# Two gathers per step of a graph-attention loop, issued behind another copy on the same engine

## The chip, the cores and the metric

The kernel runs on one core of a Trainium2 chip. A core has five engines with a queue of instructions each: PE (matrix products), DVE (elementwise work), ACT (activation functions and copies), POOL (GpSimd, which also issues the gathers) and SP (which here only issues transfers). An engine works through its queue in the order in which the program wrote it, and waits on semaphores for the others. The metric is the time of one execution on the device, in microseconds (us), lower being better. The kernel before takes 810.82 us, the median of three runs between 807.87 and 810.95.

## What is computed

Two layers of graph attention over 2048 nodes for 8 batches, a residual and two layer norms. The graph is one adjacency matrix `adj`, the same for all batches, sparse, and densest at its first nodes. Cut to what matters:

```python
def _gat_layer(h, mask, b):
    scores = jnp.einsum('...nd,...md->...nm', h, h)
    scores = jnp.where(mask, scores, NEG)
    attn = jax.nn.softmax(scores, axis=-1)
    return jnp.einsum('...nm,...md->...nd', attn, h) + b

mask = graph + jnp.eye(N) > 0
h = jnp.einsum('bnc,hdc->bhnd', x, Wh)               # B 8, N 2048, H 4 heads, D 64
out_h = _gat_layer(h, mask[None, None], bh)          # layer 1, per head
z = leaky_relu(concat_of_heads(out_h), 0.2)
h2 = jnp.einsum('bnk,dk->bnd', z, Wo)
out2 = _gat_layer(h2, mask[None], bo)                # layer 2, one head
out = layernorm(leaky_relu(out2, 0.2)) * gamma + beta
x = layernorm(x + out)
```

## The kernel before, in words

The kernel uses that the graph is sparse. The first 59 nodes (the hubs) are attended densely. The other 1989 nodes stand in 153 sets of 13. For each set a list of up to 128 neighbour nodes (one column of the tile `index`) is found on the chip from the adjacency matrix. Everything that a set needs of its neighbours is then fetched by one **gather** (`gather`, line 907; its instruction carries line 912): an indirect transfer from a table in device memory, 128 rows of 520 float32, issued by POOL, which spends its own time on it.

Before layer 1 comes a stage of dense hub work, in which the lists of the first sets are made as well. Layer 1 is the loop of line 1272. Its step `i` does two sets, 77 steps in all, software-pipelined: within one pass the work of several steps stands side by side. What matters here, in the order of the code:

- `scores(i + 1)`, line 941: PE multiplies the turned neighbours with the set's own maps; DVE subtracts the mask (line 946), ACT takes the exponential (line 953).
- `values(i)`, line 967: PE multiplies the exponentials with the gathered rows `rows[1, 2i]` and `rows[1, 2i+1]`. After it these two buffers are free. There are ten such buffers (`ROWS = 10`), so the gathers of step `i + 5` (`LOOK = 5`) use the buffers that `values(i)` has just read.
- **the two gathers** of step `i + 5`, lines 1298 to 1300.
- `own_rows`, line 920, in even steps: POOL copies the own nodes' inputs `xo`, used two steps later.
- `more(1)`, line 1318, while there are pieces left, which is in steps 0 to 9: a piece `raw` of the adjacency matrix is loaded over SP's queue (lines 776 and 778), POOL turns it to `a` (line 783) and sets a few elements (line 788, in every second step). The lists of the last 45 sets are made of these.
- `second_maps(i - 2)`, PE, line 1001; `second_rows`, `columns` and so on.
- `keep_own(i - 2)`: DVE copies the second layer's own maps out of PSUM (line 1006), and **POOL copies them into the big tile `own`** (line 1007). That tile is read in layer 2 only.
- `keep_rows(i - 3)`, DVE line 1015 and a transfer on SP's queue (line 1018) into the table of layer 2.
- the turning of the gathered rows of step `i + 3`, PE line 571 into `bank`, in two halves of four transposes with line 984 between them. This is the first reader of a gather's data. The pair issued in step `i` is thus first read at the end of step `i + 2`.

No scheduler moves anything here: the order of the code is the order on each engine. Layer 2 follows as a loop of its own with gathers from the second table. If the numbers leave the limits, a slower general kernel runs behind; it doesn't here.

Of the kernel before, what the change touches and what calls it, by code (L numbers as in the profile page):

```python
# [361 lines left out]
def fast_kernel(ctx: ExitStack, tc: tile.TileContext, x, adj, Wh, bh, Wo, bo, gamma, beta, out, flag):  # L362
# [14 lines left out]
    NG = (NS + 1) // 2  # L377
# [25 lines left out]
    def set0(g):  # L403
        return min(2 * g, NS - 2)
# [46 lines left out]
    table1 = dram.tile([N, ROW], F32, name="table1")  # L451
# [121 lines left out]
    def leaky(cat, n, name):  # L573

        z = work.tile([P, HP, 2, n], F32, tag="z", name=name, bufs=3)
        for hp in range(HP):
            nc.scalar.activation(z[:, hp], cat[:, :, hp * n:(hp + 1) * n], AF.Identity, bias=bhp[:, hp:hp + 1], scale=1.0)  # L577
        return z
# [5 lines left out]
    def project(ot, cat, n):  # L584

        for hp in range(HP):
            for s in range(2):
                for j in range(2):
                    h = 2 * hp + j
                    nc.tensor.matmul(cat[half(j), s, hp * n:(hp + 1) * n], whT[half(s), h * D:(h + 1) * D],  # L590
                                     ot[half(s), h, :], start=True, stop=True)
# [132 lines left out]
    def hub_heads(v, cat):  # L724

        for hp in range(HP):
            for s in range(2):
                for j in range(2):
                    h = 2 * hp + j
                    nc.tensor.matmul(cat[half(j), s, FREE + hp * HUB:FREE + (hp + 1) * HUB], whT[half(s), h * D:(h + 1) * D],  # L730
                                     oth[half(s), h, v * HUB:(v + 1) * HUB], start=True, stop=True)

    def keep_hub_heads(v, cat):
        for hp in range(HP):
            nc.scalar.activation(zh[:, hp, :, v * HUB:(v + 1) * HUB], cat[:, :, FREE + hp * HUB:FREE + (hp + 1) * HUB],
                                 AF.Identity, bias=bhp[:, hp:hp + 1], scale=1.0)
# [164 lines left out]
    def place(s):  # L901
        return (s + 1) % NS
# [4 lines left out]
    def gather(table, s, layer, new):  # L907
        t = rows[layer, s] = new(f"g{layer}_{s}")
        if layer == 1:
            s = set0(s // 2) + s % 2  # L910
        bound = {} if layer == 2 and place(s) < RING else dict(bounds_check=N - 1, oob_is_err=False)
        nc.gpsimd.indirect_dma_start(out=t.rearrange("n q c -> n (q c)"), out_offset=None, in_=table,  # L912
                                     in_offset=bass.IndirectOffsetOnAxis(ap=index[:, s:s + 1], axis=0), **bound)
# [20 lines left out]
    def scores(g, sp):  # L934
        xt = held.pop(("T", 1, g)).rearrange("c j (q n) -> c j q n", q=Q)
        y = held["y", g // 2][:, g % 2 * GM:(g % 2 + 1) * GM, :].rearrange("p n h -> p (n h)")
        for j in range(2):
            for q in range(Q):
                for p in range(2):
                    for r in range(2):  # L940
                        nc.tensor.matmul(sp[half(r), p, (q * 2 + j) * M:(q * 2 + j + 1) * M], xt[half(p), j, q, half(r)],  # L941
                                         y[half(p), (j * Q + q) * M:(j * Q + q + 1) * M], start=True, stop=True)

    def weigh(g, sp):
        e = es[g % 2]
        nc.vector.tensor_tensor(e[:, :16 * M].rearrange("p (a q n) -> p a q n", a=2, q=Q),  # L946
                                sp[:, :, :8 * M].rearrange("p a (q n) -> p a q n", q=Q),
                                mask[:, set0(g):set0(g) + 2, :].rearrange("p s n -> p (s n)").unsqueeze(1).unsqueeze(1)
                                .to_broadcast([P, 2, Q, 2 * M]), OP.subtract)
# [53 lines left out]
    def keep_own(g, ph):  # L1003

        t = held["own", g] = work.tile([P, GM], F32, tag="own", name=f"own{g}")
        nc.vector.tensor_copy(t, ph)  # L1006
        nc.gpsimd.tensor_copy(own[:, :, set0(g) * SET:(set0(g) + 2) * SET].rearrange("c q (j n) -> c j q n", j=2),  # L1007
                              t.rearrange("c (j q n) -> c j q n", j=2, q=Q))
# [81 lines left out]
    LOOK = 5  # L1090
# [77 lines left out]
    def one(name, tag):  # L1168
        return psum1.tile([P, 2, 512], F32, tag=tag, name=name)
# [102 lines left out]
    for i in range(-3, NG + 3):  # L1272
        if 0 <= i + 1 < NG:
            sp = one(f"s{i + 1}", "S")
            scores(i + 1, sp)
            weigh(i + 1, sp)
        cat = one(f"cat{i}", "C") if i <= NG else None
        if i > NG:
            cat = one(f"cat{i}", "S" if i == NG + 1 else "C")
        ph, pr = cat[:, 0, 384:384 + GM], cat[:GM, 1, 384:512]  # L1280
        if 0 <= i - 1 < NG:
            project(held.pop(("ot", i - 1)), cat, GM)
            if i in hub_heads_at:
                hub_heads(hub_heads_at[i], cat)
            held["z", i - 1] = leaky(cat, GM, f"z{i - 1}")
            if i in hub_heads_at:
                keep_hub_heads(hub_heads_at[i], cat)
        if 0 < i + 2 < NG:
            t = held["T", 1, i + 2] = work.tile([P, 2, 512], F32, tag="xTg", name=f"xTg{i + 2}", bufs=3)
            for k in range(2):  # L1290
                nc.scalar.copy(t[:, k, :], bank[k])  # L1291
        if 0 <= i + 1 < NG:
            lift(i + 1)
        if 0 <= i < NG:
            op = one(f"o{i}", "O")
            values(i, op)
            invert(i, op)
        if 0 <= i + LOOK < NG and i > -3:
            for j in range(2):
                gather(table1, 2 * (i + LOOK) + j, 1, rows_tile)  # L1300
        if NG - LOOK <= i < NG - 1:
            for j in range(2):
                k = 2 * (i - NG + LOOK) + j
                hub_block(k, rows_tile(f"gh{k}"))
        if i + 6 < NG and i % 2 == 0 and i >= -2:
            own_rows((i + 6) // 2)
        if i == 20:
            nc.gpsimd.memset(xbs[1], 1.0)
        if i % 2 == 0 and 0 <= (i - 30) // 2 <= NV:
            load_own((i - 30) // 2)  # L1310
        if 0 <= i - 1 < NG:
            leak(held["z", i - 1])
        if i in (4, 8):
            leak(zh)
        if i >= 0:
            if turns():
                some(1)
            more(1)
            if todo3 and i == todo3[0][0]:
                r = todo3.pop(0)[1:]  # L1320
                make_keys(*r, late_two)
                if r == (1, 1):
                    picks += pick(1)
                    done = 2 * FIRST
            if not picks:
                ready = done
            if not picks and not todo3 and done < NS:
                picks = pick(2)
                done = NS
            assert i + 1 + LOOK >= NG or set0(i + 1 + LOOK) + 1 < ready  # L1330

        if 0 <= i - 2 < NG:
            second_maps(i - 2, ph)
        if i in hub_maps_at:
            hub_maps(cat)
        if 0 <= i - 3 < NG:
            second_rows(i - 3, pr)
        if i in hub_rows_at:
            hub_rows(hub_rows_at[i], cat)
        if 0 <= i < 8:  # L1340
            hub_turn(i // 4, i % 4, cat)
        if 2 <= i + 4 < NG + NG % 2:
            columns(i + 4, cat)
            keep_columns(i + 4, cat)
        if 0 <= i < 8:
            keep_hub_turn(i % 4, cat)
        if 0 <= i - 2 < NG:
            keep_own(i - 2, ph)
        if 0 <= i - 3 < NG:
            keep_rows(i - 3, pr)  # L1350
        if i in hub_maps_at:
            keep_hub_maps(hub_maps_at[i], cat)
        if i in hub_rows_at:
            keep_hub_rows(hub_rows_at[i], cat)
        if i >= 53 and i % 2 and ahead_of_second:
            ahead_of_second.pop(0)()
        if i % 2 == 0 and 0 <= (i - 32) // 2 <= NV:
            add_beta((i - 32) // 2)
        for _ in range((2 if i < 22 or i % 2 else 1) if i >= 0 else 0):
            if not turns():  # L1360
                some(1)
        if 0 < i + 3 < NG:
            turn(bank[0], rows[1, 2 * (i + 3)])
        if 0 <= i < NG:
            turn_values(i, op)
            keep_values(i, op)
        if 0 < i + 3 < NG:
            turn(bank[1], rows[1, 2 * (i + 3) + 1])
        if NG - 3 <= i < NG:
            hub_step(i - NG + 3, bank[0])  # L1370
# [312 lines left out]
```

## Time and profile before

| what | value |
|---|---|
| median of three runs (lowest, highest) | 810.82 us (807.87, 810.95) |
| the profiled execution | 808.08 us |
| its span, first to last instruction | 806.3 us |
| PE busy | 725.3 us, 90% of the span |
| DVE, ACT, POOL busy | 585.6, 528.1, 448.4 us |
| gathers of layer 1 | 154, 1057 ns each on POOL |
| POOL's idle time before them | 166.4 us, 134.4 of it ended by line 967 on PE |
| granted TensorE clock | 0.974 |

The profile is of one execution. A row of its timeline reads: start, length, engine, line, operation, what is written and read, how many instructions are merged, and in square brackets how long the engine had been idle and what ended that. "PEld" is PE's loading of weights, which overlaps its products. A wait that is listed on an engine costs time only if that engine, or one that waits for it, sets the end.

The loop of layer 1 runs from 130.5 us (`values` of step 0) to about 546 us. In its middle a step takes 5.14 us.

### The profile page before, as it was taken

Reading aid. Unit: us, or ns where it says so; the run is one execution under the profiler, and the core shown is the slowest. Engines: PE = TensorE matmul, PEld = TensorE weight load, DVE = VectorE, ACT = ScalarE, POOL = GpSimd, SP = SyncE. Lnnn points to the kernel's source line nnn. Section 1 sums busy time; section 2 is a strip of 40 time slices with the busy share of each in tenths; the row PEclk is TensorE's granted clock in tenths of the full one; section 3 lists DMA queues with packets and bytes.
Section 4 is the critical chain, followed back from the end, with each engine's and each line's share of the span. In section 5 each row is a group of like instructions: output and inputs, shape, how many; then the busy total and the mean of one; then the engine's idle time right before and its main releaser. Section 6 shows DMA issues by size and latency. Waiting matters only on the chain.

```text
span 806.3 us, 40511 instructions
## 1 busy us (share of the span) xinstructions
PE 725.3 (90%) x17324; PEld 614.8 (76%) x17324; DVE 585.6 (73%) x1313; ACT 528.1 (66%) x1140; POOL 448.4 (56%) x622
## 2 busy tenths in 40 slices
PE   4899999999999999999999999999999899988810
PEld 3566658887889998988898999977787688876710
DVE  2558824787888878888776777664249999988883
ACT  1454646776667766666776677754668898987852
POOL 4655337667455545556554555404777777777500
PEclk9899999999999999999999999999999999999975
DMA  6889625354333334544444444435976667776521
GB/s 143 229 234 228 231 68 163 100 168 107 91 90 91 93 92 118 139 137 138 138 137 136 139 136 135 130 109 157 304 229 174 185 171 229 220 200 187 169 53 33
DMA packets 80351, 121.57 MB, mean 151 GB/s; under 512 B 34627, under 2 KB 50839, under 8 KB 80163
## 3 DMA queue, kind: packets, MB, share of 16 engines
q0 software_dynamic: 24752, 65.67, 29.5%
q1 hardware_dynamic: 52067, 52.37, 22.1%
q8 instruction: 139, 2.28, 1.1%
q10 hardware_dynamic: 3344, 0.84, 0.6%
q14 instruction: 49, 0.40, 0.2%
HBM read 116.81 MB, written 18.25 MB: 168 GB/s over the span
## 4 chain that ended last, share of the span: by engine, by line
PE 68%; DVE 12%; DMA 8%; ACT 4%; SPq 3%; issue 3%; POOL 0%; ACTq 0%; DVEq 0%; POOLq 0%
PE s L941 10%; PE o L967 10%; PE bank L571 8%; PE cat L926 6%; DMA rows<-table,index 5%; PE o L984 4%; PE cat L1001 4%; PE cat L590 4%; PE oh L693 3%; PE sh L672 3%; PE t L571 3%; PE cat L1011 2%; SPq L1529 2%; PE bank L1411 2%; DMA out_dram<-y_s 2%
## 5 line engine op out<-in xcount | busy, mean ns | idle before, releaser
L912 POOL DMA_INDIRECT g<-table,index x154 | 162.7, 1057 | 166.4 <-PE o L967 134.4
L912 POOL DMA_INDIRECT rows<-table,index x153 | 159.5, 1042 | 52.1 <-issue 17.4
L577 ACT ACTIVATE z<-cat,bhp 128x208 f32<-128x208 f32 x154 | 58.5, 431 | 98.4 <-PE cat L590 92.4
L946 DVE TENSOR_TENSOR e<-s,mask 128x832 f32<-128x832 f32 x77 | 78.6, 1020 | 25.9 <-PE s L941 24.7
L571 PE MATMUL t<-ident,rows 128*128 128x128 f32 x612 | 85.2, 278 | 10.3 <-DMA rows<-table,index 5.0
L967 PE MATMUL o<-g,e 128*64 128x65 f32 x2464 | 91.5, 225 | 3.1 <-issue 2.7
L571 PE MATMUL bank<-ident,g 128*128 128x128 f32 x608 | 91.2, 273 | 0.4 <-DVE keysi L871 0.4
L967 PEld LDWEIGHTS o<-g,e 128*64 128x64 f32 x2464 | 79.6, 137 | 14.1 <-issue 3.9
L941 PEld LDWEIGHTS s<-y,xTg 64*64 64x64 f32 x4928 | 78.9, 134 | 12.9 <-issue 12.9
L941 PE MATMUL s<-y,xTg 64*64 64x52 f32 x4928 | 88.7, 220 | 0.0
L1565 ACT COPY xts<-t 128x512 f32<-128x512 f32 x153 | 82.0, 584 | 8.7 <-PE t L571 6.9
L571 PEld LDWEIGHTS t<-ident,rows 128*128 128x128 f32 x612 | 66.6, 141 | 22.1 <-issue 7.3
L1291 ACT COPY xTg<-bank 128x512 f32<-128x512 f32 x152 | 81.7, 598 | 0.0
L953 ACT ACTIVATE e<-e,shifts 128x832 f32<-128x832 f32 x77 | 78.5, 1020 | 2.1 <-DVE e L946 2.1
L571 PEld LDWEIGHTS bank<-ident,g 128*128 128x128 f32 x608 | 72.7, 141 | 3.5 <-DVE keysi L871 1.0
L783 POOL TENSOR_SCALAR a<-raw 117x1024 bf16<-117x1024 int32 x34 | 38.8, 1143 | 51.5 <-DMA raw<-in_adj_dram 44.4
L926 PE MATMUL cat<-xo,gram 128*128 128x208 f32 (+1 forms) x304 | 65.7, 338 | 0.5 <-ACT xTg L1146 0.4
L991 ACT COPY otb<-o 128x208 f32<-128x208 f32 x154 | 43.7, 335 | 21.6 <-ACT y L932 10.2
L975 DVE TENSOR_TENSOR osb<-o,rall 128x512 f32<-128x512 f32 x77 | 53.3, 692 | 2.7
L926 PEld LDWEIGHTS cat<-xo,gram 128*128 128x128 f32 x304 | 52.5, 201 | 1.0 <-ACT xTg L1146 0.7
L974 DVE RECIPROCAL rall<-o 64x8 f32<-64x8 f32 x154 | 31.4, 204 | 25.1 <-PE o L967 23.6
L1007 POOL COPY own<-own 128x104 f32<-128x104 f32 x77 | 30.5, 396 | 29.1 <-DVE own L1006 28.9
(205 smaller groups left out, 1472.2 us busy)
## 6 DMA issues: line engine op xcount, KB each, us to landing
raw<-in_adj_dram SPq DMA_DIRECT2D x34, 432.0 KB
xr_s<-table SPq DMA_DIRECT2D x19, 256.0 KB
table<-x SPq DMA_DIRECT2D x16, 260.0 KB
table<-rowt SPq DMA_DIRECT2D x152, 26.4 KB
out_dram<-y_s SPq DMA_DIRECT2D x152, 24.0 KB
x<-in_x_dram SPq DMA_DIRECT2D x24, 128.0 KB
table<-xb SPq DMA_DIRECT2D x11, 256.0 KB
table<-share SPq DMA_DIRECT2D x10, 256.0 KB
```

The source lines that it names most:

```text
L571: nc.tensor.transpose(tp[:, q * P:(q + 1) * P], rows[:, q, 1:1 + P], ident)
L577: nc.scalar.activation(z[:, hp], cat[:, :, hp * n:(hp + 1) * n], AF.Identity, bias=bhp[:, hp:hp + 1], scale=1.0)
L912: nc.gpsimd.indirect_dma_start(out=t.rearrange("n q c -> n (q c)"), out_offset=None, in_=table, in_offset=bass.IndirectOffsetOnAxis(ap=ind ...
L926: nc.tensor.matmul(cat[:, k, :n], gram[:, g % 2 * 2 + k, :], held["x", g // 2][:, :n], start=True, stop=True)
L941: nc.tensor.matmul(sp[half(r), p, (q * 2 + j) * M:(q * 2 + j + 1) * M], xt[half(p), j, q, half(r)], y[half(p), (j * Q + q) * M:(j * Q + q ...
L946: nc.vector.tensor_tensor(e[:, :16 * M].rearrange("p (a q n) -> p a q n", a=2, q=Q), sp[:, :, :8 * M].rearrange("p a (q n) -> p a q n", q= ...
L953: nc.scalar.activation(e[:, :16 * M], e[:, :16 * M], AF.Exp, bias=shifts[:, 0:1], scale=1.0)
L967: nc.tensor.matmul(op[half(p), j, o0:o0 + K1], e[:, c0:c0 + 64], rw[j][:, q, sums(p)], start=True, stop=True)
L975: nc.vector.tensor_tensor(osb, v[:, :, :, 1:K1], r.unsqueeze(3).to_broadcast([P, 4, 2, D]), OP.mult)
L991: nc.scalar.copy(ot.rearrange("c h (p w n) -> c p h w n", p=2, w=4)[:, p], v[:, :, p * 64:p * 64 + M].rearrange("c w (n h) -> c h w n", h=H))
L1291: nc.scalar.copy(t[:, k, :], bank[k])
L1565: nc.scalar.copy(xts[pair(s) % 4][:, s % 2, :], tp)
```

## The change

The two gathers of a step are written further down in the loop's body: behind `keep_own(i - 2)` instead of directly behind `values(i)`. All else is as before.

```diff
@@ -1295,9 +1295,6 @@
             op = one(f"o{i}", "O")
             values(i, op)
             invert(i, op)
-        if 0 <= i + LOOK < NG and i > -3:
-            for j in range(2):
-                gather(table1, 2 * (i + LOOK) + j, 1, rows_tile)
         if NG - LOOK <= i < NG - 1:
...
         if 0 <= i - 2 < NG:
             keep_own(i - 2, ph)
+        if 0 <= i + LOOK < NG and i > -3:
+            for j in range(2):
+                gather(table1, 2 * (i + LOOK) + j, 1, rows_tile)
         if 0 <= i - 3 < NG:
             keep_rows(i - 3, pr)
```

Only POOL's queue is in another order. On POOL, in the middle of the loop, from the gathers of step 22 (sets 54 and 55) on, the rows were these; `g` is a gathered buffer, `xo` the own nodes' inputs, `own` the own maps:

```order
L912 DMA g_54_4799<-table_98,index 128x520
L912 DMA g_55_4803<-table_98,index 128x520
L920 COPY xo_4807<-xT 128x208
L1007 COPY own<-own_4819 128x2x4x13
L912 DMA g_56_4913<-table_98,index 128x520
L912 DMA g_57_4917<-table_98,index 128x520
L1007 COPY own<-own_4930 128x2x4x13
```

and are now:

```order
L920 COPY xo_4799<-xT 128x208
L1007 COPY own<-own_4811 128x2x4x13
L912 DMA g_54_4814<-table_98,index 128x520
L912 DMA g_55_4818<-table_98,index 128x520
L1007 COPY own<-own_4922 128x2x4x13
L912 DMA g_56_4925<-table_98,index 128x520
L912 DMA g_57_4929<-table_98,index 128x520
```

The pair of a step has gone behind the step's two copies, so it no longer stands between PE's `values` and DVE's copy of the own maps but behind both.

The second place is POOL again, in step 7, where a piece of the adjacency matrix (`raw` to `a`) lies between the old place and the new one. Sets 24 and 25 are the ones that this step gathers. Before:

```order
L912 DMA g_24_2971<-table_98,index 128x520
L912 DMA g_25_2975<-table_98,index 128x520
L783 TENSOR_SCALAR a_3_2859<-raw_3_1_2980 117x2x512
L788 AFFINE_SELECT a_3_2859<-a_3_2859 117x4
...
L1007 COPY own<-own_3012 128x2x4x13
L912 DMA g_26_3118<-table_98,index 128x520
L912 DMA g_27_3122<-table_98,index 128x520
```

and now:

```order
L912 DMA g_22_2868<-table_98,index 128x520
L912 DMA g_23_2872<-table_98,index 128x520
L783 TENSOR_SCALAR a_3_2851<-raw_3_1_2972 117x2x512
L788 AFFINE_SELECT a_3_2851<-a_3_2851 117x4
...
L1007 COPY own<-own_3004 128x2x4x13
L912 DMA g_24_3007<-table_98,index 128x520
L912 DMA g_25_3011<-table_98,index 128x520
```

Here the pair has gone behind the wait for a load from device memory as well: where the gathers of step 8 stood behind the piece, those of step 7 stand now.

## The prediction

> **What bounds the kernel now.** I read the page first, then the loop of layer 1 in stretches, then who waits for the gathers, and at last two steps row by row. The page's chain of work that ended last (the first row is its shares by engine, the second its largest lines):
>
> ```profile
> PE 68%; DVE 12%; DMA 8%; ACT 4%; SPq 3%; issue 3%; POOL 0%; ACTq 0%; DVEq 0%; POOLq 0%
> PE s L941 10%; PE o L967 10%; PE bank L571 8%; PE cat L926 6%; DMA rows<-table,index 5%; PE o L984 4%; PE cat L1001 4%; PE cat L590 4%; PE oh L693 3%; PE sh L672 3%; PE t L571 3%; PE cat L1011 2%; SPq L1529 2%; PE bank L1411 2%; DMA out_dram<-y_s 2%
> ```
>
> The gathers of layer 2 (`rows`) are on it with 5%, those of layer 1 (`g`) are not, and POOL has 0%. The stretches of layer 1 (columns: length, then busy time of PE, PE's weight loads, DVE, ACT, POOL, then clock and DMA share) say why:
>
> ```profile
> 130.50:197.50 67.00, 64.66 (x1618) 56.14 (x1610) 50.01 (x127) 44.96 (x104) 46.82 (x77) 1.00 0.45 129
> 197.50:300.00 102.50, 101.72 (x2659) 91.07 (x2654) 85.02 (x228) 71.20 (x157) 51.94 (x67) 1.00 0.34 91
> 300.00:430.00 130.00, 128.87 (x3348) 115.88 (x3345) 104.84 (x252) 89.74 (x198) 72.54 (x87) 1.00 0.48 134
> 430.00:520.00 90.00, 88.88 (x2397) 80.65 (x2391) 65.78 (x139) 62.80 (x140) 49.57 (x61) 1.00 0.49 137
> ```
>
> From 130.5 to 520 us PE is busy for 384.1 of 389.5 us. POOL has work for 220.9 us of it and idles else. So the loop is PE's own, and the change can do two things: make PE wait where it doesn't now, or take away some of the 5.4 us in which it does.
>
> Who waits for a gather's buffer, over the whole execution:
>
> ```profile
> who waited for it (us, times):
>   POOL g L912: 134.4, 68
>   DVE rall L974: 23.6, 47
>   ACT xTg L1146: 0.9, 1
> ```
>
> POOL's 134.4 us are the gathers waiting for `values` to free the buffer. No row is a reader that waited for a gather to land. In layer 1 every gather lands before PE turns it.
>
> **The change part by part.** It adds and removes no instruction; 144 gathers of the loop's 72 issuing steps (steps 0 to 71, and the pairs before it hardly) go back in POOL's queue, behind at most: half a copy `xo` per step, a piece of the adjacency matrix in steps 0 to 9, and the copy `own`. The queues of SP, DVE, ACT and PE are untouched. The cost is therefore how much later a pair is issued, against how much later it may be.
>
> *The steady step.* Step 22, an even one, with the turning of its pair two steps on:
>
> ```profile
> 258.83 1.02 POOL L912 DMA_INDIRECT g<-table,index  x1 [2.36 <-PE o L967]
> 260.16 1.07 POOL L912 DMA_INDIRECT g<-table,index  x1 [0.30 <-PE cat L926]
> 260.79 0.27 DVE L1006 COPY own<-cat 128x104 f32<-128x104 f32 x1 [0.44 <-ACT y L932]
> 261.24 0.61 POOL L920 COPY xo<-xT 128x208 f32<-128x208 f32 x1
> 261.80 0.27 POOL L1007 COPY own<-own 128x104 f32<-128x104 f32 x1
> 270.10 0.60 PE L571 MATMUL bank<-ident,g 128*128 128x128 f32 x4
> 270.93 0.60 PE L571 MATMUL bank<-ident,g 128*128 128x128 f32 x4
> ```
>
> Now the pair starts at 258.83 and 260.16. After the change `xo` runs in the 2.36 us in which POOL idled, `own` waits for DVE's copy to end (260.79 + 0.27 = 261.06), takes 0.27, and with some 0.2 for two starts (0.16 stands before the gather of 182.17 below) the pair starts at about 261.55 and, 1.33 later as now, 262.9: 2.7 us later. Read at 270.10 and 270.93, it then has 8.55 and 8.05 us to land in. How long a landing takes no row of layer 1 tells, because nobody waits there; layer 2's chain has it, from POOL's start of a gather to its landing, shortest and longest:
>
> ```profile
> 560.15 3.41 DMA rows<-table,index
> 748.04 5.41 DMA rows<-table,index
> ```
>
> By the longer one 2.6 us are left over. So in the steady steps PE waits for nothing: 0 us. What covers the 2.7 us is the lead of five steps in the buffers; were it gone, each of some 62 steps would lose up to 2.7 us, 167 in all.
>
> *The two first steps* have no `own` copy yet, and the pair still waits for `values`: nothing moves by more than a piece's work, 1.3 to 2.9 us by the two longest rows below.
>
> *Steps 4 to 9* are the tight ones, because a piece waits for its load. Step 7, whose pair is turned at the end of step 9:
>
> ```profile
> 171.91 0.84 SPq L776 DMA_DIRECT2D raw<-in_adj_dram  x1
> 172.22 1.06 POOL L912 DMA_INDIRECT g<-table,index  x1 [0.91 <-PE o L967]
> 173.59 1.03 POOL L912 DMA_INDIRECT g<-table,index  x1 [0.30 <-PE cat L926]
> 178.96 1.27 POOL L783 TENSOR_SCALAR a<-raw 117x1024 bf16<-117x1024 int32 x1 [4.34 <-DMA raw<-in_adj_dram]
> 180.20 1.59 POOL L788 TENSOR_SCALAR_AFFINE_SELECT a<-a 117x4 bf16<-117x4 bf16 x6
> 181.75 0.27 POOL L1007 COPY own<-own 128x104 f32<-128x104 f32 x1
> 182.17 1.07 POOL L912 DMA_INDIRECT g<-table,index  x1 [0.16 <-issue]
> 183.55 1.00 POOL L912 DMA_INDIRECT g<-table,index  x1 [0.30 <-PE cat L590]
> 186.03 0.60 PE L571 MATMUL bank<-ident,g 128*128 128x128 f32 x4
> 186.87 0.60 PE L571 MATMUL bank<-ident,g 128*128 128x128 f32 x4
> ```
>
> The load of line 776 is issued in SP's queue, which doesn't change, and lands 7.05 us later, at 178.96. Behind it come line 783, six of line 788 and `own`, and then, where step 8's pair stands now (182.17 and 183.55), step 7's: 10 us later than before. PE wants it at 186.03 and 186.87. With a landing of 3.41 us the first is there at 185.58, in time, and the second at 186.96, 0.1 late. With 5.41 the first comes at 187.58, 1.55 late; that moves the second's turn to 188.42, and it comes at 188.96, 0.54 late: 2.1 us. I take the middle, 1.1 us. PE has no slack in this loop, so it is lost once.
>
> In the other load steps each pair likewise starts where the next step's starts now, as long as the load decides. Step 6's would start about 171.5, behind its `own` copy, and is turned at 179.76; step 9's, the tightest of them, about 193.5, and is turned at 199.85:
>
> ```profile
> 171.03 0.28 POOL L1007 COPY own<-own 128x104 f32<-128x104 f32 x1
> 179.76 0.60 PE L571 MATMUL bank<-ident,g 128*128 128x128 f32 x4
> 192.76 0.58 POOL L1007 COPY own<-own 128x104 f32<-128x104 f32 x1
> 199.85 0.60 PE L571 MATMUL bank<-ident,g 128*128 128x128 f32 x4
> ```
>
> They have 8.3 and 6.3 us, over 5.41: nothing lost. Nor does the delay pile up, since step 8's pair stands behind its own piece at about 187.0, where step 9's stands now.
>
> The Trainium skill, "DMA: Bandwidth & Descriptors", section "Anatomy of one DMA — SWDGE (gpsimd) path", fits such a transfer as 2.0 us plus its bytes over 436e3 per us. For 128 rows of 520 float32 that is an estimate of 2.6 us behind POOL's 1.07; the pair would land at 185.8 and 187.2, and the loss would be 0.3 us in place of 1.1. The layer 2 rows run from 0.3 us below that 3.7 to 1.7 above it, so I stay with them.
>
> *What is gained.* The pieces and `own` come earlier, and `own` is read in layer 2 only. Nothing on PE's side waits for either: 0 us.
>
> **The sum**: 0 (steady steps) + 0 (steps 0 to 6, 8, 9) + 1.1 (step 7) = 1.1 us, between 0.1 and 2.1, on the profiled execution's 808.08. The median of the runs stands 2.7 us above that execution, and the runs lie at both ends; I add the 1.1 to the middle of the two (809.45) and predict 810.6 us. What a measurement of this kernel can tell from no change is about 0.5%, 4 us: this is "no change".
>
> **The rivals.**
>
> *No stall at all.* In step 7 the load now shares the transfers with the gathers of 172.22 and 173.59. If it lands 1 to 2 us earlier because step 6's pair, which comes in their place, is out of the way sooner, the pair of step 7 makes it. For it: 7.05 us against 3.41 to 5.41 for a gather looks like crowding. Against: step 6's pair moves into about the same moment (171.5). Time: 809.45, again "no change".
>
> *Slower: the load's crowd falls on the pair behind it.* Place: step 7's gathers, issued when SP issues the next piece's load at 182.51. If they take as long as the load of 171.91, 7.05 us, the first lands at 189.22, 3.2 us late, and the second at 190.60, 0.5 after its moved turn (190.06): 3.7 us. It decides against "no change" when the landing exceeds 7.05 by 0.3, or when step 6's pair, with 8.3 us, is hit as well. With 1 us more at both that is about 5.5 us, 815. For it: the one long wait for a load that POOL has. Against: only 1 step of 72 stands like this.
>
> *Faster: DVE gets time back.* DVE's line 1054 adds two SBUF tiles and runs beside POOL's copies (groups of 300 to 540 us, then one that runs beside neither copy):
>
> ```profile
> L1054 DVE TENSOR_TENSOR xb<-xb,bet 128x512 f32<-128x512 f32 x11 | 10.8, 979 | 0.8 <-DMA share<-in_x_dram 0.4
> L1054 DVE TENSOR_TENSOR share<-share,bet 128x512 f32<-128x512 f32 x10 | 9.3, 926 | 0.3
> 397.53 0.69 DVE L1054 TENSOR_TENSOR xb<-xb,bet 128x512 f32<-128x512 f32 x1
> ```
>
> The copies will mostly be over by then, and 11 × 0.29 + 10 × 0.24 = 5.6 us of DVE's time come free. That would be 803.9 if the DVE bound the loop. The Trainium skill, "SBUF — State Buffer", section "Who interferes with whom", says that a DVE instruction with two SBUF inputs contends with a GpSimd instruction that reads SBUF; by that rule these rows should shorten to the undisturbed length. But PE's waits in the loop, three of 0.4 us or less left out, are these:
>
> ```profile
> PE o L967 <- issue: 2.7, 4, 1.1
> PE o L984 <- DVE osb L975: 1.6, 3, 0.6
> PE cat L1001 <- ACT share L735: 1.3, 4, 0.3
> PE cat L1001 <- ACT z L577: 1.0, 1, 1.0
> ```
>
> DVE ends 1.6 us of them. So at most that, and more than 4 us only together with something that I don't see.
>
> *The change doesn't do what it says* only in steps 0 and 1, as worked out.
>
> **How the numbers follow.** The forecast (one short stall in step 7) has 0.55, no stall 0.25; both are within 0.5%. The slower one has 0.13, and a gain of over 4 us 0.07, mostly because the runs of before themselves lie 3 us apart. So faster 0.07, same 0.80, slower 0.13. The range: below, 807, a run from the lower end of before's (807.87) with a gain under 1 us; above, 815, the top run (810.95) with the 3.7 us of the slower rival.
>
> **What would show it.** In the changed profile the steady step is still 5.14 us, with POOL's pair starting 2.7 us later, behind line 1007. POOL's idle time ended by line 967 falls from 134.4 us to a few, and the wait of line 1007 for DVE's line 1006 grows in its place. Line 1054 comes down towards 0.69 us. PE's waits gain one row, `bank` of line 571 waiting for a transfer into `g`, of 0.1 to 2.1 us near 186 us, and no other. I am wrong if that row stands at many steps or adds up to over 4 us, or if PE's step in the middle of the loop is no longer 5.14 us.

## The result and the profile after

The changed kernel takes **839.84 us** (median of four runs, 838.56 to 841.27), against 810.88 for the kernel before beside it (807.87 to 814.43): a ratio of **1.0341 [1.0295, 1.0386]** (in brackets the 95% interval), 3.4% slower; the quotient of the two medians alone is 1.036. Forecast were 810.6 us and "no change". Ratios here and below leave out runs that took over 1.5% longer than the fastest of their kernel, up to 853.46 us at a clock of 0.84, while the medians have them all.

The profiled execution has a span of 837.1 us, 30.8 more than before. In every view below, rows in between are left out. These are the stretches of layer 1 in the middle of the loop (length, then busy time and count of PE, PE's weight loads, DVE, ACT, POOL, then clock and DMA share):

```profile
197.50:300.00 102.50, 98.50 (x2472) 86.36 (x2471) 79.17 (x214) 64.66 (x143) 47.40 (x63) 1.00 0.33 83
300.00:430.00 130.00, 125.58 (x3116) 110.85 (x3120) 95.22 (x240) 82.38 (x183) 59.64 (x81) 1.00 0.45 121
```

PE is still "busy" 96% of the time, but it does fewer products in it: 2472 and 3116, where it did 2659 and 3348. The clock is 1.00 as before. So PE's time has been stretched, mostly under its busy time: over the 232.5 us its products fell by 7%, which is some 16 us' worth, and its idle time grew by 6.5 us. From the first product of one step's scores to the first of the next, a step without other work took 5.14 us; now most take about 5.4 or 5.8, often in turns. Over the whole loop, first scores to last, that is 406.9 us before and 435.7 after: 28.8 of the 30.8 us.

Two groups of the page of after, and what PE waits for between 130.5 and 576 us (total, times, longest):

```profile
L1007 POOL COPY own<-own 128x104 f32<-128x104 f32 x77 | 22.7, 295 | 167.6 <-DVE own L1006 167.6
L577 ACT ACTIVATE z<-cat,bhp 128x208 f32<-128x208 f32 x154 | 58.3, 430 | 128.3 <-PE cat L590 118.6
```

```profile
PE cat L1001 <- ACT z L577: 8.2, 22, 1.0
PE bank L571 <- DMA g<-table,index: 2.3, 1, 2.3
```

A wait for a gather's data stands there once. PE's line 1001 now waits at 22 places for ACT's line 577 (once before, 1.0 us), and ACT's line 577 itself idles until PE's line 590. A steady step shows why. After the change (start, length, engine, line, what; in brackets the idle time before and what ended it):

```profile
280.02 0.27 POOL L1007 COPY own<-own 128x104 f32<-128x104 f32 x1 [1.72 <-DVE own L1006]
280.10 1.15 PE L941 MATMUL s<-y,xTg 64*64 64x52 f32 x64
280.80 1.03 POOL L912 DMA_INDIRECT g<-table,index  x1 [0.51 <-issue]
281.07 0.55 PE L590 MATMUL cat<-otb,whT 64*64 64x104 f32 x16
281.68 1.02 DVE L946 TENSOR_TENSOR e<-s,mask 128x832 f32<-128x832 f32 x1 [1.20 <-PE cat L590]
282.00 0.76 ACT L577 ACTIVATE z<-cat,bhp 128x208 f32<-128x208 f32 x2 [1.62 <-PE cat L590]
282.81 0.58 PE L1001 MATMUL cat<-z,woT 128*64 128x104 f32 x8
```

And before:

```profile
261.19 1.15 PE L941 MATMUL s<-y,xTg 64*64 64x52 f32 x64
262.17 0.55 PE L590 MATMUL cat<-otb,whT 64*64 64x104 f32 x16
262.44 1.02 DVE L946 TENSOR_TENSOR e<-s,mask 128x832 f32<-128x832 f32 x1 [0.33 <-PE s L941]
262.78 0.76 ACT L577 ACTIVATE z<-cat,bhp 128x208 f32<-128x208 f32 x2 [1.31 <-PE cat L590]
263.63 0.54 PE L1001 MATMUL cat<-z,woT 128*64 128x104 f32 x8
```

Counted from the first product of the scores: DVE's line 946 started at 1.25 us and now at 1.58, ACT's line 577 at 1.59 and now at 1.90, PE's line 1001 at 2.44 and now at 2.71. PE's own products of lines 941 and 590 start no later here. What comes later is their end as the others are told of it. The semaphore that the last product of the scores raises came 263 ns behind that product's start before, and comes 657 ns behind it now (medians between 200 and 520 us). By then line 590 has run too, so that the profile names it as what DVE's line 946 waited for. In other steps the products of line 590 themselves are spread. Worked out from all steps between 200 and 520 us, the mean time from the first product of a part to the first of the next:

```
part of a step         before    after
scores, L941           972 ns    981 ns
projection, L590       485       631
values, L967          1090      1348   (with the wait of L1001 behind it)
the rest              2740      2740
step                  5287      5699
```

The loss sits in the two parts beside and behind which the gather now starts, 0.7 us behind the scores' first product.

### The profile page after: what moved, and what is told of

It is laid out like the page before. It is cut to its first block, busy times and chain, and to the rows that moved or that the text cites. A ratio compares the mean times of both kernels' runs of the same rounds, so it can differ in the third digit from the quotient of the medians.

```text
span 837.1 us, 40540 instructions
## 1 busy us (share of the span) xinstructions
PE 744.7 (89%) x17324; PEld 624.4 (75%) x17324; DVE 579.9 (69%) x1313; ACT 526.4 (63%) x1140; POOL 437.1 (52%) x622
## 4 chain that ended last, share of the span: by engine, by line
PE 66%; DMA 9%; DVE 9%; ACT 7%; SPq 3%; issue 3%; POOL 0%; DVEq 0%; POOLq 0%; ACTq 0%
PE s L941 10%; PE bank L571 8%; PE cat L590 7%; PE cat L926 6%; PE cat L1001 4%; ACT z L577 4%; PE o L967 4%; PE o L984 4%; PE oh L693 3%; DMA rows<-table,index 3%; PE t L571 3%; PE sh L672 3%; SPq L1529 3%; PE cat L1011 2%; DMA out_dram<-y_s 2%
## 5 line engine op out<-in xcount | busy, mean ns | idle before, releaser
L912 POOL DMA_INDIRECT g<-table,index x154 | 158.1, 1027 | 65.2 <-issue 44.7
L946 DVE TENSOR_TENSOR e<-s,mask 128x832 f32<-128x832 f32 x77 | 78.7, 1022 | 48.2 <-PE s L941 26.5
L1007 POOL COPY own<-own 128x104 f32<-128x104 f32 x77 | 22.7, 295 | 167.6 <-DVE own L1006 167.6
L941 PE MATMUL s<-y,xTg 64*64 64x52 f32 x4928 | 90.4, 221 | 0.0
L1001 PE MATMUL cat<-z,woT 128*64 128x104 f32 x616 | 43.7, 263 | 11.5 <-ACT z L577 8.2
L1006 DVE COPY own<-cat 128x104 f32<-128x104 f32 x77 | 20.5, 266 | 47.3 <-ACT y L932 42.2
```

The source lines that it names most:

```text
L1001: nc.tensor.matmul(dst, woT[:, hp, :], src, start=(hp == 0), stop=(hp == HP - 1))
```

## The experiments

Letters of theories are explained in each expectation. Added gathers, memsets and moves stand in steps 10 to 71, 62 of them; where an expectation says 66, or 57 gathers, that is a slip. In the kernels of some runs a line has moved down by one or more: 942 is then 941, and so on. The first four ran on one chip, on which the kernel before takes 813.12 us (808.72 to 820.01); ratios are always to the kernel before on the same chip.

**The pair a little later still.** Three memsets, 1.04 us together, between the own copy and the pair:

```diff
             keep_own(i - 2, ph)
+        if 10 <= i < NG - LOOK:
+            for _ in range(3):
+                nc.gpsimd.memset(filler, 0.0)
         if 0 <= i + LOOK < NG and i > -3:
```

> The changed kernel, but from step 10 on POOL fills three small tiles (about 0.97 us) between its copy of the own maps and the pair of gathers, so that the pair comes still later. Theory A, position: what costs is a gather whose issue on POOL begins while PE is at the end of the scores (line 941) or in the projection (line 590), because PE is held there; shifted by 1 us the pair lies beside line 967 and behind, and the steady step goes back to 5.14 us: 811 to 816 us. Theory B, lateness: the pair's later issue as such costs, so later still costs more: 850 us or above. Theory C, the copy of the own maps ahead of the pair costs by itself: about 840 us, as the changed kernel.

Measured: 819.22 us, ratio 1.0039 [1.0002, 1.0077]. A step, between its scores at 336.32 and 341.45:

```profile
336.32 1.15 PE L942 MATMUL s<-y,xTg 64*64 64x52 f32 x64
336.47 1.04 POOL L1349 MEMSET filler<- 128x256 f32 x3
337.91 0.76 ACT L578 ACTIVATE z<-cat,bhp 128x208 f32<-128x208 f32 x2 [1.31 <-PE cat L591]
337.98 1.04 POOL L913 DMA_INDIRECT g<-table,index  x1 [0.47 <-PE cat L591]
341.45 0.74 PE L942 MATMUL s<-y,xTg 64*64 64x52 f32 x36
```

5.13 us (the view ends within the second scores, so their row is cut short). ACT's line starts 1.59 us behind the scores, as before the change. Gathers that come **later** still cost almost nothing, so it isn't lateness; and a POOL that works beside the scores, on memsets, does no harm. The time is 3 us above what the theory of the place allowed; the loop's own total in the profile is 416.2, with the excess in single steps and not in the steady ones.

**Half of the change.** The gathers behind `own_rows` and the piece of the adjacency matrix, but ahead of `second_maps` and `keep_own`:

```diff
+        if 0 <= i + LOOK < NG and i > -3:
+            for j in range(2):
+                gather(table1, 2 * (i + LOOK) + j, 1, rows_tile)
         if 0 <= i - 2 < NG:
             second_maps(i - 2, ph)
```

> Half of the change: the pair is issued behind the copy xo and behind the piece of the adjacency matrix, but still ahead of the copy of the own maps. Theory A, position: in the steady steps the pair starts where it did before, beside PE's lines 1001 to 984, and only the load steps keep their delay (one wait of about 2 us in step 9): 811 to 815 us. Theory D, the load steps carry the loss: about 840 us. Theory C, the copy ahead of the pair: 811 us.

Measured: 815.25 us, ratio 1.0025 [0.9983, 1.0067], steady step 5.14. The pair then starts 2.8 us behind the scores, where it stood before. Being behind the load of a piece costs little: the loop takes 408.6 us in this profile, against 406.9 in that of before. The rest of the loss hangs on being behind the own copy.

**A third gather, its result not read,** at the place of the changed kernel, in the kernel before (whose own pair stays):

```diff
             keep_own(i - 2, ph)
+        if 10 <= i < NG - LOOK:
+            nc.gpsimd.indirect_dma_start(out=spare_rows, out_offset=None,
+                in_=table1.rearrange("n (a c) -> (n a) c", a=2),
+                in_offset=bass.IndirectOffsetOnAxis(ap=index[:, 0:1], axis=0),
+                bounds_check=N - 1, oob_is_err=False)
```

> The kernel before, with its pair in the old place, and in steps 10 to 71 a third gather of half a row's width behind the copy of the own maps, whose result nobody reads. Theory A, position: this gather meets lines 941 and 590 of PE as the pair does in the changed kernel, and each of 62 steps loses 0.3 to 0.5 us: 829 to 842 us. Theory B, lateness of the data: nothing that is read is late, 811 to 813 us.

Measured: 832.13 us in two runs, ratio 1.0224 [1.0137, 1.0310], 2.2% slower; the interval excludes no loss, but not a loss under 2%. Two steps, the third gather (line 1351) at two places:

```profile
280.76 1.15 PE L942 MATMUL s<-y,xTg 64*64 64x52 f32 x64
281.46 1.03 POOL L1351 DMA_INDIRECT spare_rows<-table,index  x1 [0.50 <-issue]
282.66 0.76 ACT L578 ACTIVATE z<-cat,bhp 128x208 f32<-128x208 f32 x2 [1.62 <-PE cat L591]
286.20 1.15 PE L942 MATMUL s<-y,xTg 64*64 64x52 f32 x64
...
336.31 1.15 PE L942 MATMUL s<-y,xTg 64*64 64x52 f32 x64
337.89 0.76 ACT L578 ACTIVATE z<-cat,bhp 128x208 f32<-128x208 f32 x2 [1.31 <-PE cat L591]
339.57 1.04 POOL L1351 DMA_INDIRECT spare_rows<-table,index  x1 [3.06 <-issue]
341.44 0.74 PE L942 MATMUL s<-y,xTg 64*64 64x52 f32 x36
```

The first step, with the gather 0.70 us behind its scores' start, takes 5.44 us, and ACT's line starts at 1.90 as in the changed kernel; the second, with the gather at 3.26, takes 5.13, with ACT at 1.58. Of all steps between 200 and 520 us, the 39 with the third gather at 0.5 to 1.3 us have a median of 5.60, the 15 with it at 1.3 to 1.7 us one of 5.24. The loss follows the place of the gather, and since nobody reads this one, no reader of its data can be what PE waits for.

**The same with a plain transfer** of POOL's in place of the gather:

```diff
+            nc.gpsimd.dma_start(out=spare_rows, in_=table1[:P, :ROW // 2])
```

> As the run with the third gather, but the third transfer is a plain one of 128 rows in a row, issued by POOL at the same place, with no list of indices. Theory A1, any transfer that POOL issues there holds PE: 829 to 842 us. Theory A2, only the gather with its list does: 811 to 814 us.

Measured: 818.01 us, ratio 1.0032 [0.9984, 1.0081], steady step 5.14:

```profile
339.25 1.15 PE L942 MATMUL s<-y,xTg 64*64 64x52 f32 x64
339.69 0.59 POOL L1351 DMA_DIRECT2D spare_rows<-table  x1
340.84 0.76 ACT L578 ACTIVATE z<-cat,bhp 128x208 f32<-128x208 f32 x2 [1.31 <-PE cat L591]
```

A plain transfer of the same size, issued by POOL in the middle of the scores, delays nothing. In 27 steps between 190 and 520 us it starts 0.5 to 1.3 us behind them, around the place of the gather, and their median is 5.14. So it is the gather with its list that costs PE's time, and not any transfer that POOL issues.

**On another chip.** The next runs fell on a chip on which the kernel before takes 954.46 us (948.08 to 964.98). Three vary the third gather: directly behind the pair; of 16 rows; behind 1.2 us of memsets.

```diff
+            nc.gpsimd.indirect_dma_start(out=spare_rows[:16], out_offset=None, ...
+                in_offset=bass.IndirectOffsetOnAxis(ap=index[:16, 0:1], axis=0), ...
```

> The same third gather, issued directly behind the pair in its old place, so that its issue begins with the scores (line 941), about a microsecond before the projection, in steps 10 to 71. If the scores themselves are held, each step loses 0.3 us or more: 829 us and above. If only their end and the projection are, the steady step stays at 5.14 to 5.25 us: below 820 us.

> The third gather behind the copy of the own maps again, where it cost 0.36 us a step, but of 16 rows in place of 128. If the hold is a fixed cost of a gather's issue: steady step about 5.5 us, +2%. If it scales with the rows (the list that is read, the descriptors that are written): 5.14 to 5.2 us, within 0.7%.

> The third gather of the earlier run once more, at half a row's width and read by nobody, but behind about 1 us of small fills on POOL, so that its issue begins beside PE's line 967 and not beside lines 941 and 590. It moves the same bytes as the run with the third gather did. Position: steady step 5.14 us, not over 0.7% above the kernel before. Traffic or POOL's extra work: the 2% of that run stay.

Measured: behind the pair 1035.88 us, ratio 1.0847 [1.0785, 1.0909]; 16 rows 1047.34, 1.0967 [1.0902, 1.1031]; behind memsets 1017.1, 1.065 [1.0583, 1.0718]. All three cost far more than expected. On this chip PE stops within the scores, waiting for nothing that the profile names. The run behind the pair tells from when to when: between 200 and 520 us, of the stretches of over 0.3 us from one product's start to the next one's, 47 begin about 0.19 us behind the start of a gather and end about 0.90 behind it, and 39 run from 1.01 to 1.65 (medians). PE's own instruction fetches don't fit: the last one ended anywhere from 0.1 to 7.1 us ahead of PE's going on.

**A piece converted one step later,** in the kernel before, since its steps 8 to 10 have gathers beside the small products too. The conversion is put off by one call:

```diff
-                load_adj(*pieces.pop(0))
+                converts.append(load_adj(*pieces.pop(0)))
+            while len(converts) > later[0]:
+                converts.pop(0)()
```

> A version meant to be faster than both: the kernel before, with the gathers in the old place, but in steps 0 to 9 POOL converts each piece of the adjacency matrix one step after its load was issued, so that it doesn't stand waiting for the load and the pairs of steps 8 and 9 come in time, not beside lines 941 and 590 of PE. Position: the steps that in the kernel before last 6.43, 6.28 and 8.68 us lose about 0.6 to 1 us each, some 2 to 3 us in all, 0.3%. If these steps are long for another cause: no change.

Measured, on the same chip: 953.26 us, ratio 0.9984 [0.9953, 1.0016]. No gain that can be measured; the interval holds both the 0.3% expected and none.

**Place, rows, number, half a pair.** From the stops grew theory W. Its four runs fell on a third chip, again one with a slow kernel before (954.49 us, 952.08 to 963.6). The first has 0.5 us of memsets ahead of the pair of the changed kernel; two repeat kernels from above; the last leaves the first gather of a pair in its old place:

```diff
-            for j in range(2):
+            for j in range(1 if 10 <= i else 2):
                 gather(table1, 2 * (i + LOOK) + j, 1, rows_tile)
...
             keep_own(i - 2, ph)
+        if 10 <= i < NG - LOOK:
+            gather(table1, 2 * (i + LOOK) + 1, 1, rows_tile)
```

> The kernel after, with about 0.5 us of memsets on POOL between the own copy and the pair in steps 10 to 66, so that the first gather of a pair should start some 1.2 us behind the first product of the scores instead of 0.7. Theory W (windows): a gather holds PE's instructions from about 0.2 to 0.9 us and again from about 1.0 to 1.65 us behind its own start, and only the two groups of small products (scores, projection, together 0 to 1.46 us of a step) feel it. Then the first hold begins at 1.4, when the projection's last products (at 1.3) have begun: step 5.14 to 5.25, ratio to the kernel before of the same chip 1.000 to 1.012. Rival: it is the start of the gather beside the small products that counts; 1.2 is still inside the projection: step 5.4 or more, ratio over 1.018.

> The kernel before, with a third gather of 16 rows in place of 128 behind the own copy in steps 10 to 66, its result not read; the same kernel as the one with sixteen rows above, in the hope of a chip like the first. Theory W: the hold belongs to the gather, not to its rows: step 5.4 to 5.6, ratio 1.015 to 1.035, as with 128 rows (1.022). Rival: it goes with the rows: an eighth of that, ratio under 1.006.

> The kernel before, with a third gather of 128 rows behind some 1.2 us of small memsets behind the own copy in steps 10 to 66, so at about 1.6 to 2.0 us of a step; the same kernel as the shifted one above. Theory W: nothing small is near: step 5.14 to 5.2, ratio under 1.008, though the chip works off 57 gathers more. Rival: every further gather costs wherever it stands, as the runs on the second chip read at first: step 5.4 to 5.5, ratio 1.018 or more.

> The change half done: in steps 10 to 66 the first gather of a pair stays behind the values, the second goes behind the own copy. Theory W: the second gather of the changed kernel starts at 2.0 us and holds nothing small, so one gather at 0.7 us costs what the pair costs: step 5.5 to 5.8, ratio 1.02 to 1.035. Rival: each gather of the pair bears half of the loss: step 5.3 to 5.45, ratio 1.010 to 1.018.

Measured: memsets ahead of the pair 1139.0 us, ratio 1.187 [1.1779, 1.1961]; 16 rows 1039.74, 1.0839 [1.0755, 1.0922]; the third gather behind memsets 1019.92, 1.0656 [1.0577, 1.0734]; half a pair 1001.59, 1.0449 [1.037, 1.0529]. All four lie above what theory W expected, the first by far, and its groups between 200 and 520 us say how:

```profile
L968 PE MATMUL o<-g,e 128*64 128x65 f32 x1278 | 66.2, 238 | 25.3 <-issue 25.1
L942 PE MATMUL s<-y,xTg 64*64 64x52 f32 x2560 | 50.8, 222 | 5.7 <-issue 5.7
```

With the scores over, the stops fall on `values`, whose 32 products theory W had counted as safe. And half a pair costs 4.5% where a whole pair costs 18.5% on a fourth chip (below): with a second gather behind the first the stops go on.

**All on one chip.** The last four kernels ran on a fourth chip (before 941.5 us, 938.12 to 948.35): the change itself, the third gather with 128 rows, with 16, and with 128 behind memsets.

> The changed kernel once more, beside the three kernels below on one chip. On a chip that runs the kernel before in about 811 us: ratio 1.030 to 1.040 as measured. On one that runs it in about 954 us a gather was seen to hold PE's products two times or more for some 0.65 us each, not once for 0.2 to 0.4: theory W then expects at least twice the loss, ratio 1.08 to 1.20.

> The kernel before with a third gather of 128 rows behind the own copy, its result not read. Theory W on the fast chip: ratio 1.022 as measured before. On the slow chip: as with 16 rows there (1.084 to 1.097), within 0.02, because the hold belongs to the gather. Rival: the hold goes with the rows: clearly over 1.10 there.

> The same with 16 rows. Theory W on the fast chip: 1.015 to 1.030, as with 128 rows; the rival (it goes with the rows): under 1.006. On the slow chip 1.08 to 1.10 as before.

> The third gather of 128 rows behind 1.2 us of memsets. Theory W on the fast chip: under 1.008, step 5.14 to 5.2; the rival (every further gather costs wherever it stands): as the run of 128 rows without memsets. On the slow chip 1.06 to 1.07 as before, and below the two runs without memsets by 0.015 or more.

Measured: the change 1118.56 us, ratio **1.1851** [1.1773, 1.193]; 128 rows 1030.18, 1.0924 [1.0851, 1.0997]; 16 rows 1028.61, 1.0904 [1.0828, 1.098]; shifted 1010.62, 1.0696 [1.0619, 1.0773]. All four lie in what theory W expected of such a chip. So 16 rows cost what 128 cost: the hold belongs to the gather.

The shifted run doesn't say what a gather away from the scores costs. Its third gather starts 3.07 us behind the scores (median) and not at 1.6 to 2.0, and it pushes the kernel's own pair back: in 15 of 54 steps a gather of the pair starts less than 1.5 us behind the next scores' start. Steps with any gather from 0.7 us ahead of that start to 1.5 behind it have a median of 7.09 us there, the others 5.99, and the steps of the run with the later conversion, without a third gather, 5.45. So part of its 7% is again the place, of other gathers. The changed kernel on this chip:

```profile
329.63 1.50 PE L941 MATMUL s<-y,xTg 64*64 64x52 f32 x60
330.22 1.02 POOL L912 DMA_INDIRECT g<-table,index  x1 [0.51 <-issue]
331.51 0.34 PE L941 MATMUL s<-y,xTg 64*64 64x52 f32 x4 [0.38 <-issue]
331.55 1.00 POOL L912 DMA_INDIRECT g<-table,index  x1 [0.30 <-issue]
331.63 0.27 PE L590 MATMUL cat<-otb,whT 64*64 64x104 f32 x1
332.25 0.42 PE L590 MATMUL cat<-otb,whT 64*64 64x104 f32 x5 [0.35 <-issue]
332.98 0.51 PE L590 MATMUL cat<-otb,whT 64*64 64x104 f32 x10 [0.31 <-issue]
333.42 1.15 PE L967 MATMUL o<-g,e 128*64 128x65 f32 x32
```

Behind the pair PE gets 4, 1, 5, 10 products through at a time, a go every 0.73 us, where in the profile of before all 16 of line 590 took 0.55 us. It is "issue": no semaphore ends these stops. Over the whole execution line 590 has

```profile
L590 PE MATMUL cat<-otb,whT 64*64 64x104 f32 x1232 | 90.6, 268 | 44.5 <-issue 44.4
```

44.5 us of idle time ahead of it. On the first kind of chip the same thing would be small enough to hide under "busy" PE and a late semaphore; that it is the same is argued, not shown.

The 18.5% isn't the stops alone. In this profile TensorE's granted clock fell to half in 24 stretches of 3.4 us within the loop, 81.9 of its 595.8 us, where the loops of the kernel before and of the changed kernel on the first chip have none. That can account for at most 41 us, half of the 81.9, of the 177 lost. Steps without such a stretch have a median of 7.53 us, those with one 9.07. The run with memsets ahead of the pair has 29 such stretches, the runs with a third gather three at most, the half-done change none.

**What stays open.** What in a gather's work on POOL stops PE isn't shown: neither its data (16 rows), nor the issue of a transfer as such (plain transfer), nor POOL being busy (memsets), nor PE's instruction fetch fits. All of these times come from executions that were profiled, so whether an unprofiled kernel is held the same way isn't shown either. Why the kernel before itself takes 941 to 954 us on these three chips stays open; the run with the later conversion has 423 us in layer 1 there against 406.9, so most of it lies elsewhere: 387.5 us behind the last scores against 272.8. Layer 2, which has gathers of its own, lies there, and PE's products of line 1411 (1417 in that run's kernel) idle 19.7 us for "issue" in that run, against none before. That would fit the same hold, and isn't shown. Whether 16 rows cost as much as 128, and whether a whole third gather behind memsets is free, no run shows for a chip like the first.

## Why the prediction was wrong

**The step that failed** is the first term of the sum: "So in the steady steps PE waits for nothing: 0 us." It was worked out from the landing of the data alone. That half was right: from 195 us on, by the gathers' semaphores, the data were there 4 us or more ahead of their reader for all but five gathers, and 2.3 us at the least, and a third gather that nobody reads costs two thirds as much (2.2% against 3.4%). But the change also moves the issue itself, from beside PE's long products to 0.7 us behind the start of its scores, and the issue costs PE's time there. Of the 28.8 us that the loop lost, 2.3 lie in its first 12 steps, with the stall of step 7; the other 26.5 lie in the 64 steps behind them, 0.41 us each. The unread third gather alone cost 0.31 (19.0 us over 62 steps). No rival had it: all four asked what POOL's order does to transfers and copies, none what POOL's gather does to an engine that doesn't wait for it.

**The trace of before had shown it.** The load of a piece delays the pairs of steps 8 and 9, so that their gathers stand beside these products. The rows of 182.17 and 183.55 were quoted for their starts only; beside them and a step later stand

```profile
182.58 1.58 PE L967 MATMUL o<-g,e 128*64 128x65 f32 x32
188.37 0.72 PE L590 MATMUL cat<-otb,whT 64*64 64x104 f32 x16
188.41 1.00 POOL L912 DMA_INDIRECT g<-table,index  x1 [0.30 <-issue]
190.44 1.03 PE L967 MATMUL o<-g,e 128*64 128x65 f32 x27 [0.77 <-issue]
```

where line 967 takes 1.15 in an undisturbed step and line 590 0.55. The semaphore at the scores' end came 1150 and 1123 ns behind the last product's start there, against 263. That the gathers are the cause there is read from the likeness: the later conversion, which puts these gathers back behind `values`, gained nothing that could be measured, though in its profile, on a chip whose other steps are longer, the three steps take 6.59, 5.60 and 7.75 us in place of 6.43, 6.28 and 8.68.

**The pair's new start** came 3.07 us later (0.70 + 5.14 - 2.77, behind the scores) and not 2.7, since 0.51 us go by between the copy and the first gather. As foreseen, POOL's idle time ended by `values` fell, from 134.4 to 1.8 us, and the wait of line 1007 for line 1006 grew to 167.6.

**Step 7** stalled, once, and no other step did; that mechanism was right and its size short, 2.3 us against 1.1 (0.1 to 2.1):

```profile
183.86 1.07 POOL L912 DMA_INDIRECT g<-table,index  x1 [0.17 <-PE cat L590]
189.40 0.63 PE L571 MATMUL bank<-ident,g 128*128 128x128 f32 x4 [2.33 <-DMA g<-table,index]
```

From the gather's start to PE's go 5.5 us passed, about the longest of the rows that the forecast took (5.41) and not their middle, and PE wanted the data 3.2 us behind the gather's start, not 3.9. The estimate by the Trainium skill ("DMA: Bandwidth & Descriptors", "Anatomy of one DMA — SWDGE (gpsimd) path") lies lower still: its 2.6 us are the page's for a whole transfer, setup and completion included, and even behind POOL's 1.07, where the prediction put them, they make 3.7. That no other step stalled was in part luck: the second gather of step 6, started at 174.29 us, took 7.2 us to land by its semaphore, as the rival of the crowd had it, and was there 0.24 us before PE read it. That rival's upper sum is a little off: with a landing 1 us longer its own rows give 4.7 us for step 7 and 0.3 for step 6, 5.1 in all and not 5.5.

**The faster rival's premise held, its gain didn't.** DVE's line 1054 on `xb` fell from 979 to 692 ns now that POOL's copies run beside it for 0.1 us at the most in the usual step and not for the whole of it, as the trace of before and the rule of the Trainium skill had it ("SBUF — State Buffer", "Who interferes with whom"):

```profile
L1054 DVE TENSOR_TENSOR xb<-xb,bet 128x512 f32<-128x512 f32 x11 | 7.6, 692 | 0.8 <-DMA share<-in_x_dram 0.4
```

DVE has 5.7 us less to do in all (585.6 to 579.9), and the loop, which DVE doesn't bound, got nothing of it. The rival of crowded transfers (3.7 to 5.5 us) had the right sign for a reason that cost 2.3 us of the 28.8.

The sign named for being wrong was a step no longer at 5.14 us, and that is what came.

## What to carry to other kernels

When an instruction moves, ask not only who waits for its result but what it will now run beside, and look in the trace for a place where it already stands like that: here two steps of the kernel before did, and showed the price. Keep gathers away from stretches in which PE works through many small products, and look at a late semaphore or a stretched "busy" group, not only at waits. Time such a change on more than one chip: this one cost 3.4% on one and 18.5% on another.

## What the runs showed of the hardware

A gather issued by GpSimd costs the time of TensorE, which waits for nothing of it. On the first chip the signal of the scores' end came 0.66 us behind the last product in place of 0.26, and steps grew from 5.14 to 5.4 to 5.8 us. On another, in the changed kernel, PE stopped from 0.22 to 0.64 us and from 0.77 to 1.40 behind a gather's start (medians of 72 and 77 stretches of over 0.3 us from product to product, between 200 and 520 us). There 16 rows did it as 128 did (1.0904 and 1.0924); on the first kind of chip a plain transfer and memsets of GpSimd didn't (1.0032 and 1.0039). The Trainium skill, "SBUF — State Buffer", "Who interferes with whom", says of the engines' ways into SBUF that PE and ACT never wait on anyone; that these stops come by way of SBUF isn't shown, so the runs don't contradict it; taken more widely, that nothing of GpSimd's can cost PE time, it would not hold here.

The chips differ by far more than their runs do: the kernel before took 811 us beside the changed kernel and 813 on the chip of the first experiments, but 941 to 954 on three other chips, each time within 2% of itself.
